# Second routed layer of a graph network on one core: weight loads, bias products, result copies and a norm in other places

## The chip, the cores and the metric

The kernel runs on one core of a Trainium2 chip. The metric is the device time of the whole kernel in microseconds, 5201.13 before the change (median of 3 runs, 5199.01 to 5203.52). A core has five engines that run side by side: TensorE (PE, matmuls and transposes, weights loaded by LDWEIGHTS), VectorE (DVE), ScalarE (ACT), GpSimd (POOL) and SyncE (SP). In this kernel SP issues DMAs only, ACT issues some beside its own work, and POOL issues the indirect ones, which gather rows by a list of indices. Every engine works through its own instructions in order.

## The reference, cut to what matters

Eight layers, alternating graph layers and feed-forward layers, act on 625 nodes of 512 features, each adding to x. The change lies in the fourth, `_L1_ffn_ref`, a routed layer in two levels:

```python
gw = _topk_gate(x @ wg_group, GK, G)              # 2 of 4 groups for each node
z = _layernorm(x, ln_g, ln_b)
out = jnp.zeros_like(x)
for g in range(G):
    iw = _topk_gate(z @ wg_inner[g], EK, E)       # 2 of 8 experts in each group
    moe = jnp.zeros_like(z)
    for e in range(E):
        h = jax.nn.relu(z @ W1[g, e] + b1[g, e])
        moe = moe + iw[:, e:e + 1] * (h @ W2[g, e] + b2[g, e])
    y = _layernorm(z + moe, gln_g[g], gln_b[g])
    out = out + gw[:, g:g + 1] * y
return out.reshape(b, t, d) + inp
```

So each node has four places: two groups, and two experts in each. There are 32 experts, W1 is 512 x 128 and W2 128 x 512 for each, all f32.

## The kernel before, in words

A node is a row; 625 rows are five tiles of 125 (`NT`, `P`). `L1_ffn` has these stages.

Inputs and gates. `C.normed` makes xin, the layer's input; `C.layernorm` makes z, which goes to DRAM as `nodes1` (rows to be gathered). `C.feature_major` (line 166) turns xin and z into xT and zT: four PE transposes a tile into PSUM, and a copy to SBUF that `C.copy` (line 176) gives to DVE and ACT in turn (even tiles DVE, odd tiles ACT). Gate products on xT (pg) and zT (pi), the two best of each (`top8`), and a ranking follow. They give `who` (for every expert a list of up to 128 rows), `to` (where each node finds its four results), and gT, the gates turned so that a product with the biases gives a tile's bias part. A branch (line 1210) on the largest list leads to `L1_late` for lists that are too long; it isn't taken here.

Bias products. For each tile three PE products with gT: one with the norms' biases (line 1223), added to x by DVE (line 1225), after POOL has added xin (line 1224); and for each j, the lower and the upper of a node's two groups, one with b2 (line 1228), added to z by DVE as zb[j] (line 1229). They have 8 or 32 rows of weights and 512 columns.

Experts. Expert e passes through three steps. `places(e)`: rows gathered by POOL (`fetch`, six experts ahead) are transposed by PE (line 1237) and copied to xg (line 1239, ACT). `first(e)`: eight PE matmuls with W1 (line 1249), then relu with bias to hid (line 1251, ACT). `second(e)`: two PE matmuls with W2 to y in PSUM (line 1257), a copy to ys (line 1259, DVE), and a store to `made` in DRAM (line 1260, SP). Each pass of the loop runs `places(e + 1)`, `first(e)`, `second(e - 1)`.

Weights. Four experts' W1, or their W2, are one part of 1 MB; 16 parts pass through a ring of six buffers (`RING`). `load(upto)` issues on SP all parts up to a number. Six are issued ahead of the loop; `first` and `second` ask for more with every expert, which matters at the first of four. A load into a buffer waits on SP until the last matmul that reads the buffer is done.

Results. Once the first 24 experts are stored, `take(0)` gathers the rows of the lower groups on POOL (ten indirect DMAs, line 1269), and `norm(0, ...)` weighs and adds them to zb[0] (line 1280), takes mean and variance (1281, 1282), a square root on ACT, multiplies by the norms' gains from PE (1291, 1292) and adds to x (1293). After the last expert `take(1)` and `norm(1, ...)` do so for the upper groups, in parts of two, two and one tiles, and `C.seen(t)` starts the next layer's norm.

Order. The program's order is the text's, but a scheduler at build time arranges each engine's instructions: one that is ready in its model may be set ahead of earlier ones. In this kernel it set the POOL adds of line 1224 (759.8 us) ahead of the gates, and one gain product of `norm(0)` (844.1 us) ahead of the first expert. Tiles of a name share a number of buffers (`bufs`): xg, hid and ys three each, the PSUM tiles pt, ph, y and pg two each.

Of the kernel before, what the change touches and what calls it, by code (L numbers as in the profile page):

```python
# [15 lines left out]
F32 = mybir.dt.float32  # L16
# [12 lines left out]
N, D, P, NT = 625, 512, 125, 5  # L29
KC = D // 128  # L30
# [10 lines left out]
SLOTS = 128  # L41
RING = 6
# [6 lines left out]
class Ctx:  # L49
# [113 lines left out]
                nc.vector.scalar_tensor_tensor(dst[:, t], src[:, t], mv[:, t, 0:1], g[:P], op0=ALU.subtract, op1=ALU.mult)  # L163
                nc.vector.scalar_tensor_tensor(dst[:, t], dst[:, t], r[:, t:t + 1], b[:P], op0=ALU.mult, op1=ALU.add)

    def feature_major(self, ps, dst, src):

        nc = self.nc
        for t in range(NT):
            pt = ps.tile([128, 512], F32, name="pt")  # L170
            for k in range(KC):
                nc.tensor.transpose(pt[:, k * P:(k + 1) * P], src[:, t, k * 128:(k + 1) * 128],
                                    self.ident[:P, :P])
            self.copy(t, dst[:, :, t * P:(t + 1) * P], pt[:, :KC * P].rearrange("p (k n) -> p k n", k=KC))

    def copy(self, turn, dst, src):

        if turn % 2:
            self.nc.scalar.copy(dst, src)
        else:  # L180
            self.nc.vector.tensor_copy(dst, src)
# [823 lines left out]
def L1_ffn(C):  # L1005
# [7 lines left out]
    nc, tc, I = C.nc, C.tc, C.ins  # L1013
    G, EX, NG = 4, 8, 5
    ALL = G * EX
    W = lambda name: I["L1_ffn_" + name]
    with ExitStack() as st:
# [4 lines left out]
        parts = [(g, q, n) for g in range(G) for q in range(2) for n in ("W1", "W2")]  # L1022
        loaded = {}

        def load(upto):

            for key in parts[len(loaded):upto]:
                g, q, n = key
                w = ring.tile([128, 4, 512], F32, name="ring")
                src = W(n)[g, 4 * q:4 * q + 4]  # L1030
                if n == "W1":
                    nc.sync.dma_start(w, src.rearrange("e (p k) h -> p e (k h)", p=128))
                else:
                    nc.sync.dma_start(w, src.rearrange("e h d -> h e d"))
                loaded[key] = w
# [5 lines left out]
        xin = pool.tile([P, NT, D], F32, name="xin")  # L1041
        C.normed(xin)
        z = pool.tile([P, NT, D], F32, name="z")
# [3 lines left out]
        zT = pool.tile([128, KC, N], F32, name="zT")  # L1047
# [18 lines left out]
        gT = pool.tile([128, N], F32, name="gT")  # L1066

        rb, gb = R([128, D], "rb"), R([128, D], "gb")
# [7 lines left out]
        to = pool.tile([P, 4, NT], U32, name="to")  # L1076
# [4 lines left out]
        def fetch(e):  # L1081
            fetched[e] = at_pool.tile([SLOTS, D], F32, name="at_e")
            nc.gpsimd.indirect_dma_start(out=fetched[e], out_offset=None, in_=nodes[:, :],
                                         in_offset=bass.IndirectOffsetOnAxis(ap=who[:, e:e + 1], axis=0))

        with tc.tile_pool(name="c_ps", bufs=2, space=PSUM) as ps, tc.tile_pool(name="c_x", bufs=1) as xpool:
# [1 line left out]
            wide = R1([P, NT, 4, 32], "wide")  # L1088
            nc.gpsimd.memset(wide, 0.0)
            xT = xpool.tile([128, KC, N], F32, name="xT")  # L1090
            C.feature_major(ps, xT, xin)
            C.feature_major(ps, zT, z)
            wg = pool.tile([128, KC, G], F32, name="wg")
            nc.scalar.dma_start(wg, W("wg_group").rearrange("(k p) g -> p k g", p=128))
            wi = pool.tile([128, KC, G, EX], F32, name="wi")
# [2 lines left out]
            for t in range(NT):  # L1098
                pg = ps.tile([P, G], F32, name="pg", bufs=1)
# [6 lines left out]
            n = NT * NG  # L1106
# [44 lines left out]
            for c in range(4):  # L1151
                for t in range(NT):
                    nc.vector.tensor_scalar(at[:, c, t], slots, rk[:, c, t:t + 1], None, op0=ALU.is_equal)
                    nc.tensor.matmul(pw.rearrange("s h e -> s (h e)"), at[:, c, t], named[:, c, t].rearrange("p h e -> p (h e)"),
                                     start=(c, t) == (0, 0), stop=(c, t) == (3, NT - 1))
# [30 lines left out]
            for t in range(NT):  # L1186
                pt = ps.tile([128, 512], F32, name="pt")
# [25 lines left out]
        work = E(tc.tile_pool(name="c_work", bufs=3))  # L1213
# [3 lines left out]
        ps_g = E(tc.tile_pool(name="c_ps_g", bufs=2, space=PSUM))  # L1217

        zb = [work.tile([P, NT, D], F32, name=f"zb{j}", bufs=1) for j in range(2)]
        for t in range(NT):  # L1220
            cols = slice(t * P, (t + 1) * P)
            po = ps_g.tile([P, D], F32, name="pg")
            nc.tensor.matmul(po, gT[64:64 + 2 * G, cols], gb[64:64 + 2 * G], start=True, stop=True)
            nc.gpsimd.tensor_add(C.x[:, t], C.x[:, t], xin[:, t])
            nc.vector.tensor_add(C.x[:, t], C.x[:, t], po)
            for j in range(2):
                po = ps_g.tile([P, D], F32, name="pg")
                nc.tensor.matmul(po, gT[32 * j:32 * j + 32, cols], rb[32 * j:32 * j + 32], start=True, stop=True)
                nc.vector.tensor_add(zb[j][:, t], z[:, t], po)
        state = {}  # L1230

        def places(e):

            pt = ps_t.tile([128, KC, SLOTS], F32, name="pt")
            rows = fetched.pop(e).rearrange("s (p k) -> s k p", k=KC)
            for k in range(KC):
                nc.tensor.transpose(pt[:, k], rows[:, k], C.ident[:SLOTS, :SLOTS])
            state[e] = work.tile([128, KC, SLOTS], F32, name="xg")
            nc.scalar.copy(state[e], pt)
            if e + 6 < ALL:  # L1240
                fetch(e + 6)

        def first(e):
            g, ex = divmod(e, EX)
            load(parts.index((g, ex // 4, "W1")) + 1 + RING)
            w1 = loaded[g, ex // 4, "W1"]
            ph = ps_h.tile([128, SLOTS], F32, name="ph")
            for k in range(KC):
                nc.tensor.matmul(ph, w1[:, ex % 4, k * 128:(k + 1) * 128], state[e][:, k], start=k == 0, stop=k == KC - 1)
            state[e] = work.tile([128, SLOTS], F32, name="hid")  # L1250
            nc.scalar.activation(state[e], ph, AF.Relu, bias=b1[:, e:e + 1])

        def second(e):
            g, ex = divmod(e, EX)
            load(parts.index((g, ex // 4, "W2")) + 1 + RING)
            y = ps_y.tile([128, D], F32, name="y")
            nc.tensor.matmul(y[:SLOTS], state.pop(e), loaded[g, ex // 4, "W2"][:, ex % 4], start=True, stop=True)
            ys = work.tile([128, D], F32, name="ys")
            nc.vector.tensor_copy(ys[:SLOTS], y[:SLOTS])
            nc.sync.dma_start(made[DENSE + e * SLOTS:DENSE + (e + 1) * SLOTS], ys[:SLOTS])  # L1260

        rows = {}
# [1 line left out]
        def take(j):  # L1264
            rows[j] = [work.tile([P, NT, D], F32, name=f"r{i}", bufs=1) for i in range(2)]
            upto = DENSE + (ALL - EX * (1 - j)) * SLOTS
            for t in range(NT):
                for i in range(2):
                    nc.gpsimd.indirect_dma_start(out=rows[j][i][:, t], out_offset=None, in_=made[:upto, :],
                                                 in_offset=bass.IndirectOffsetOnAxis(ap=to[:, 2 * i + j, t:t + 1], axis=0))  # L1270

        def norm(j, ts):

            a, b = ts[0], ts[-1] + 1
            st_ = C.small.tile([P, NT, 6], F32, name="ln_st")
            mv = C.small.tile([P, NT, 2], F32, name="ln_mv")
            moe = zb[j]
            for t in ts:
                for i in range(2):
                    nc.vector.scalar_tensor_tensor(moe[:, t], rows[j][i][:, t], score[:, 2 * i + j, t:t + 1], moe[:, t], op0=ALU.mult, op1=ALU.add)  # L1280
                nc.vector.bn_stats(st_[:, t], moe[:, t])
                nc.vector.bn_aggr(mv[:, t], st_[:, t])
            v = C.small.tile([P, NT], F32, name="ln_v")
            nc.vector.tensor_scalar_add(v[:, a:b], mv[:, a:b, 1], EPS)
            r = C.small.tile([P, NT], F32, name="ln_r")
            C.rsqrt(r[:, a:b], v[:, a:b], [P, b - a])
            nc.vector.tensor_mul(r[:, a:b], r[:, a:b], wj[:, j, a:b])
            for t in ts:
                gain = ps_g.tile([P, D], F32, name="pg")
                k = 64 + 32 * j  # L1290
                nc.tensor.matmul(gain, gT[k:k + G, t * P:(t + 1) * P], rb[k:k + G], start=True, stop=True)
                nc.vector.scalar_tensor_tensor(moe[:, t], moe[:, t], mv[:, t, 0:1], gain, op0=ALU.subtract, op1=ALU.mult)
                nc.vector.scalar_tensor_tensor(C.x[:, t], moe[:, t], r[:, t:t + 1], C.x[:, t], op0=ALU.mult, op1=ALU.add)

        places(0)
        for e in range(ALL + 1):
            if e + 1 < ALL:
                places(e + 1)
            if e < ALL:
                first(e)  # L1300
            if e:
                second(e - 1)
            if e == ALL - EX + 1:
                take(0)
            if e == ALL - 2:
                norm(0, range(NT))
        take(1)
        for ts in ((0, 1), (2, 3), (4,)):
            norm(1, ts)
# [638 lines left out]


PHASES = [graph_and_L0_gnn, L0_ffn, L1_gnn, L1_ffn, L2_gnn, L2_ffn, L3_gnn, L3_ffn]  # L1950


# [48 lines left out]
```

## Time and profile before

| | us |
|---|---|
| median of three runs | 5201.13 |
| the profiled execution's own time | 5200.93 |
| its span in the profile | 5199.1 |
| layer: end of the layer before to x's last tile | 757.4 to 993.4 |
| PE busy in the whole span | 4803.9 (92%) |
| DVE, ACT, POOL busy | 2679.2, 1098.0, 122.1 |
| DMA, mean over the span | 47 GB/s |

Most of the span is a later layer, a recurrence of 625 steps, which starts after this one is done; the share of busy PE over the whole span therefore says little about this layer. Groups of instructions in the layer: x is the number, us the busy time, ns the mean of one.

| line, engine, what | x | us | ns |
|---|---|---|---|
| 1257 PE y | 64 | 39.5 | 717 |
| 1249 PE ph | 256 | 38.2 | 294 |
| 1237 PE pt | 128 | 22.3 | 300 |
| 1228 and 1223 PE bias products | 20 and 10 | 16.3 and 10.3 | 1132 and 1133 |
| 1259 DVE ys | 32 | 21.8 | 690 |
| 1239 ACT xg | 32 | 18.8 | 587 |
| 1251 ACT hid | 32 | 11.8 | 368 |
| 1083 POOL gathers of rows | 32 | 30.6 | 957 |
| 1269 POOL gathers of results | 20 | 25.0 | 1248 |

A matmul in f32 is two instructions. In the profile's lists, "a <-b" after an idle time names what ended it; a wait row reads: engine, tile and line that waited, what it waited for, us in total, times, the longest. SPq is SP's queue of DMAs, and a DMA's row is the time that SP took to issue it.

### The profile page before, as it was taken

The numbers are of one execution on the slowest core, as the hardware profiler recorded it, in microseconds if no ns is written. First come the engines' busy times: TensorE is split into PE (matmuls) and PEld (weight loads), VectorE is DVE, ScalarE is ACT, GpSimd is POOL, SyncE is SP. The second block draws the span as 40 slices with busy tenths as digits, with TensorE's granted clock in tenths as the row PEclk, the third lists the DMA queues.
The fourth block names the chain that finished last, engine by engine and source line by source line (L and its number), as shares of the span: only waits on it lengthen the run. The fifth ranks groups of instructions, "written<-read, shape, count | busy, mean of one in ns | idle before, by whom it ended". The sixth has DMA issues, their size and how long they took to land. (4 is left out here: it accounts for less than half of the span.)

```text
span 5199.1 us, 184513 instructions
## 1 busy us (share of the span) xinstructions
PE 4803.9 (92%) x74204; PEld 3035.4 (58%) x74204; DVE 2679.2 (52%) x13548; ACT 1098.0 (21%) x4475; POOL 122.1 (2%) x120
## 2 busy tenths in 40 slices
PE   8998977799999799999999999999999999999988
PEld 6566745455567455555555555555555555555555
DVE  7533043400161366666656666665666656656258
ACT  8442111110151111111111111111111111111124
POOL 0100012200000000000000000000000000000000
PEclk9998986799899899999999999999999999999988
DMA  1223954311163100000000000000000000000200
GB/s 38 74 97 128 317 181 163 117 51 47 45 214 124 60 6 6 6 6 6 6 6 13 6 6 6 6 6 6 6 6 6 6 6 6 6 6 0 71 13 11
DMA packets 163039, 246.84 MB, mean 47 GB/s; under 512 B 67001, under 2 KB 67374, under 8 KB 162124
## 3 DMA queue, kind: packets, MB, share of 16 engines
q1 hardware_dynamic: 144480, 221.36, 13.0%
q0 software_dynamic: 8800, 16.92, 1.1%
q10 hardware_dynamic: 9594, 6.59, 0.5%
q8 instruction: 76, 1.25, 0.1%
q14 instruction: 89, 0.73, 0.0%
HBM read 198.90 MB, written 45.91 MB: 47 GB/s over the span
## 5 line engine op out<-in xcount | busy, mean ns | idle before, releaser
L1699 PE MATMUL pa<-wp,left 128*23 128x384 bf16 x33312 | 1499.0, 328 | 126.6 <-issue 38.5
L1699 PEld LDWEIGHTS pa<-wp,left 128*23 128x23 bf16 x33312 | 794.8, 93 | 653.0 <-DVE left L1836 152.1
L1728 PE MATMUL po<-wo,left 128*1 128x128 f32 x20000 | 656.1, 273 | 0.0
L1728 PEld LDWEIGHTS po<-wo,left 128*1 128x1 f32 x20000 | 475.4, 84 | 133.3 <-issue 0.3
L1740 PE MATMUL spare<-wo,ident 128*128 128x256 f32 x1250 | 437.9, 432 | 25.6 <-issue 25.6
L1804 DVE COPY col<-gxb 128x16 f32 x625 | 114.4, 183 | 648.3 <-DVEq L1779 648.3
L1814 DVE STREAM_TRANSPOSE col<-pa 128x384 f32<-128x384 f32 x625 | 349.6, 559 | 190.7 <-PE pa L1699 190.7
L1771 ACT ACTIVATE act<-ga 128x12 f32<-128x12 f32 x625 | 132.6, 212 | 1178.1 <-DVE ga L1816 1178.1
L1766 ACT COPY xrow<-xsb 1x4 f32<-1x4 f32 x625 | 120.5, 193 | 1214.2 <-ACTq L1764 1214.2
L1740 PEld LDWEIGHTS spare<-wo,ident 128*128 128x128 f32 x1250 | 186.2, 188 | 166.3 <-issue 166.3
L1541 PE MATMUL pg<-xT,w 128*128 128x312 f32 (+1 forms) x1024 | 274.4, 429 | 0.8 <-DVE gt L1550 0.3
L1541 PEld LDWEIGHTS pg<-xT,w 128*128 128x128 f32 x1024 | 194.1, 190 | 80.7 <-DVE gt L1550 3.2
L1691 PE MATMUL lg<-wso,th 128*1 128x8 f32 x5008 | 216.1, 169 | 15.5
L1687 PE MATMUL lg<-wsel,act 128*1 128x8 f32 x5008 | 219.2, 169 | 2.1 <-DVE act L1825 0.9
L1818 DVE STREAM_TRANSPOSE col<-po 128x128 f32<-128x128 f32 x625 | 198.2, 317 | 26.6 <-PE po L1728 1.2
L1691 PEld LDWEIGHTS lg<-wso,th 128*1 128x1 f32 x5008 | 148.2, 81 | 74.1 <-DVE wso L1828 13.5
L1684 PEld LDWEIGHTS lg<-xrow,ones 1*1 1x1 f32 x1252 | 51.3, 76 | 238.8 <-issue 238.8
L502 PE MATMUL wide<-hot_dst,hot_src 125*125 125x512 bf16 x640 | 177.0, 389 | 13.3 <-DVE hot_dst L482 12.9
L1828 DVE TENSOR_TENSOR wso<-wsel,so 128x32 f32<-128x32 f32 x625 | 120.3, 192 | 117.6 <-ACT so L1773 115.9
L1687 PEld LDWEIGHTS lg<-wsel,act 128*1 128x1 f32 x5008 | 149.4, 81 | 48.1 <-DVE act L1825 3.3
L232 PE MATMUL po<-w,hT 128*125 128x512 f32 x400 | 175.1, 592 | 0.0
L1773 ACT ACTIVATE so<-go 128x4 f32<-128x4 f32 x625 | 128.3, 205 | 216.8 <-DVE go L1823 216.8
(495 smaller groups left out, 5905.4 us busy)
## 6 DMA issues: line engine op xcount, KB each, us to landing
ring<-in_L_ffn_W_dram SPq DMA_DIRECT2D x80, 1024.0 KB
gxb<-gx SPq DMA_DIRECT2D x25, 800.0 KB
w<-in_L_ffn_WihT_dram SPq DMA_DIRECT2D x16, 1024.0 KB
raw<-in_L_ffn_WhhT_dram SPq DMA_DIRECT2D x24, 512.0 KB
gx<-gt SPq DMA_DIRECT2D x16, 626.0 KB
made<-ys SPq DMA_DIRECT2D x39, 256.0 KB
gx<-gt SPq DMA_DIRECT2D x16, 624.0 KB
w<-in_L_gnn_Wl_dram SPq DMA_DIRECT2D x8, 1024.0 KB
```

Of the source, the lines that this page charges most:

```text
L232: self.nc.tensor.matmul(out, xT[:, k, t * P:(t + 1) * P], w[:, k, :], start=start and k == 0, stop=stop and k == k_n - 1)
L502: nc.tensor.matmul(wide[i], hs[:, k], hd[:, :W0], start=first, stop=last)
L1541: nc.tensor.matmul(pg[:, :n], w[:, k, s * 128:(s + 1) * 128], xT[:, k, n0:n0 + n], start=k == 0, stop=k == KC - 1)
L1687: pe.matmul(lg, c2[:, s:s + 1], wsel[:, 1, s], start=False, stop=False)
L1691: m = pe.matmul(lg, th[:, s:s + 1], wso[:, s], start=False, stop=s == KC - 1)
L1699: m = pe.matmul(pa[32 * j:32 * j + 2 * GAP + 1], upper[:, s], wp[e][:, s, i, j].rearrange("p g n -> p (g n)"), start=k == 0, stop=k == 11, ...
L1728: m = pe.matmul(po[32 * j:32 * j + 1].rearrange("p (u r) -> p u r", r=32), left[:, s, 0:1], wo[e][:, s].rearrange("p (u j r) -> p j u r", ...
L1740: pe.matmul(spare[:, :256], C.ident, wo[0][:, 0, :256], start=True, stop=True)
L1771: act.activation(act4[:, 0:3].rearrange("p g s -> p (g s)"), ga, AF.Tanh, scale=0.5).then_inc(sem["ifg"])
L1773: act.activation(so, go, AF.Sigmoid).then_inc(sem["so"])
L1814: dve.transpose(col[:, :12, :32], pa.rearrange("p (b r) -> p b r", r=32)).then_inc(sem["ta"])
L1818: dve.transpose(col[:, 12:, :32], po.rearrange("p (s r) -> p s r", r=32)).then_inc(sem["to"])
```

## The change

- `load` is asked for `RING - 1` in place of `1 + RING` parts beyond the number of the part in use: at part number i, parts up to i + 4 are issued where it was up to i + 6.
- The bias products become a function `inputs(i)` that does one product; the loop calls it once in each pass from e = 2 to 16, after `second`. The order within a tile is b2 of both j first, then the norms' biases.
- The copy to ys goes from DVE to ACT, the copy to xg from ACT to DVE; xg has two buffers in place of three, ys four in place of three.
- The ten copies of `feature_major` in this layer are all on ACT.
- `norm(0, range(NT))` becomes `norm(0, (0, 1))` at the same place and `norm(0, (2, 3, 4))` after the last `second`.

```diff
-    def feature_major(self, ps, dst, src):
+    def feature_major(self, ps, dst, src, copy=None):
...
-            self.copy(t, dst[:, :, t * P:(t + 1) * P], pt[:, :KC * P].rearrange("p (k n) -> p k n", k=KC))
+            to, of = dst[:, :, t * P:(t + 1) * P], pt[:, :KC * P].rearrange("p (k n) -> p k n", k=KC)
+            copy(to, of) if copy else self.copy(t, to, of)
...
-            C.feature_major(ps, xT, xin)
-            C.feature_major(ps, zT, z)
+            C.feature_major(ps, xT, xin, nc.scalar.copy)
+            C.feature_major(ps, zT, z, nc.scalar.copy)
...
-        for t in range(NT):
+
+        def inputs(i):
+            t, what = divmod(i, 3)
             cols = slice(t * P, (t + 1) * P)
             po = ps_g.tile([P, D], F32, name="pg")
-            nc.tensor.matmul(po, gT[64:64 + 2 * G, cols], gb[64:64 + 2 * G], start=True, stop=True)
-            nc.gpsimd.tensor_add(C.x[:, t], C.x[:, t], xin[:, t])
-            nc.vector.tensor_add(C.x[:, t], C.x[:, t], po)
-            for j in range(2):
-                po = ps_g.tile([P, D], F32, name="pg")
+            if what == 2:
+                nc.tensor.matmul(po, gT[64:64 + 2 * G, cols], gb[64:64 + 2 * G], start=True, stop=True)
+                nc.gpsimd.tensor_add(C.x[:, t], C.x[:, t], xin[:, t])
+                nc.vector.tensor_add(C.x[:, t], C.x[:, t], po)
+            else:
+                j = what
                 nc.tensor.matmul(po, gT[32 * j:32 * j + 32, cols], rb[32 * j:32 * j + 32], start=True, stop=True)
                 nc.vector.tensor_add(zb[j][:, t], z[:, t], po)
...
-            state[e] = work.tile([128, KC, SLOTS], F32, name="xg")
-            nc.scalar.copy(state[e], pt)
+            state[e] = work.tile([128, KC, SLOTS], F32, name="xg", bufs=2)
+            nc.vector.tensor_copy(state[e], pt)
...
-            load(parts.index((g, ex // 4, "W1")) + 1 + RING)
+            load(parts.index((g, ex // 4, "W1")) + RING - 1)
...
-            load(parts.index((g, ex // 4, "W2")) + 1 + RING)
+            load(parts.index((g, ex // 4, "W2")) + RING - 1)
...
-            ys = work.tile([128, D], F32, name="ys")
-            nc.vector.tensor_copy(ys[:SLOTS], y[:SLOTS])
+            ys = work.tile([128, D], F32, name="ys", bufs=4)
+            nc.scalar.copy(ys[:SLOTS], y[:SLOTS])
...
             if e:
                 second(e - 1)
+            if 2 <= e < 17:
+                inputs(e - 2)
             if e == ALL - EX + 1:
                 take(0)
             if e == ALL - 2:
-                norm(0, range(NT))
+                norm(0, (0, 1))
+            if e == ALL:
+                norm(0, (2, 3, 4))
```

## The prediction

> **What bounds the kernel now.** I read the page first, then cut the second routed layer into four stretches, then read its chain of work in order of time, last its table of waits and the DMA queue's own waits. The layer's last result (x of the fifth tile) stands at 993.4 us of a span of 5199.1; everything after it waits for x, so what the layer saves, the kernel saves. The four stretches run from the last norm of the layer before (757.4), the first row transposes after the branch (824.65), the expert loop (842.42) and the last store of an expert's result (957.9):
>
> ```profile
> 757.40:824.65 67.25, 36.72 (x156) 29.37 (x156) 45.60 (x221) 4.76 (x10) 15.34 (x17) 0.52 0.48 148
> 824.65:842.42 17.77, 16.57 (x25) 6.07 (x26) 8.48 (x13) 0.00 (x0) 0.00 (x0) 0.50 0.00 1
> 842.42:957.90 115.48, 91.45 (x455) 64.39 (x455) 34.26 (x58) 32.03 (x66) 36.62 (x36) 0.84 0.73 241
> 957.90:993.40 35.50, 13.08 (x15) 3.56 (x13) 29.86 (x98) 1.20 (x7) 12.89 (x10) 0.50 0.31 88
> ```
>
> Columns: length, busy time of PE, weight load, DVE, ACT, POOL, granted clock, DMA share, GB/s. The second stretch is nothing but bias products, with DMA idle. In the third PE is idle 24 us and its clock falls. Where the loop is smooth, an expert takes 2.22 us (857.92 to 860.15 to 862.37):
>
> ```profile
> 857.92 1.02 PE L1257 MATMUL y<-ring,hid 128*128 128x512 f32 x2
> 858.78 0.63 PE L1237 MATMUL pt<-ident,at_e 128*128 128x128 f32 x4
> 859.25 1.06 PE L1249 MATMUL ph<-xg,ring 128*128 128x128 f32 x8
> 860.15 1.02 PE L1257 MATMUL y<-ring,hid 128*128 128x512 f32 x2
> ...
> 862.37 1.02 PE L1257 MATMUL y<-ring,hid 128*128 128x512 f32 x2
> ```
>
> 32 x 2.22 is 71 us, not 115. The waits of the loop say why:
>
> ```profile
> DVE ys L1259 <- DMA made<-ys: 42.5, 10, 12.5
> PE y L1257 <- DVE ys L1259: 18.7, 8, 6.1
> SPq L1260 <- DVE ys L1259: 89.4, 20, 38.3
> SPq L1034 <- PE y L1257: 17.1, 4, 7.8
> SPq L1032 <- PE ph L1249: 12.7, 5, 4.9
> ```
>
> The copy of y waits 42.5 us for an earlier store to leave its buffer. Stores and weights share SP's queue, and a weight load stands there until the block that now uses its ring buffer is done (12.7 and 17.1 us). Seen in time:
>
> ```profile
> 864.79 0.38 SPq L1032 DMA_DIRECT2D ring<-in_L_ffn_W_dram  x1
> 873.03 0.38 SPq L1034 DMA_DIRECT2D ring<-in_L_ffn_W_dram  x1
> 873.51 1.77 SPq L1260 DMA_DIRECT2D made<-ys  x3
> ```
>
> Three stores stand behind the load of 873.03. (Of the 89.4 us, 38.3 are only the wait for the first result.)
>
> **What the skill says.** "DMA: Bandwidth & Descriptors", section "Anatomy of one DMA — SWDGE (gpsimd) path": a semaphore wait is made on the issuing sequencer before dispatch. The trace agrees: everything behind the waiting load is late. Same page, "Issuing engines are not separate DMA queues": transfers of all queues share 16 engines. It agrees: from 858 to 866 loads, stores and row gathers fill them (share 0.97, 325 GB/s). "ScalarE: Activation LUTs", section "Table sets: the hidden batching unit": relu and copy lie in every set, so copies cost no table load. It agrees: the layer has one load for Exp and one for Sqrt, none for Relu or copy. "TensorE: Matmul & The Clock Gate", section "What's actually happening": the clock is halved unless PE has been busy; it agrees (0.50 at 825 to 842, 1.00 at 858 to 866), with a twist used below.
>
> **The change, part by part**, against the profiled execution: 5200.93 us, that is 1.8 outside its span, and 0.2 under the median 5201.13.
>
> Loads. Place q used to ask for the part six ahead, into the buffer in use; now four ahead, into the buffer of two places before, which the last instructions have just freed. The load starts at the same moment as before, but SP no longer stands on it. Nothing is loaded later. With one more result buffer (4), the 42.5 us wait loses its cause. What stays is the store's own way: the one issued at 859.4 behind two loads of 1 MB still held a buffer until about 870.1, some 10.7 us. Four buffers at 3.1 us each (below) give 12.4. It just fits while bias products are in the loop; at 2.22 us (8.9) it is short by 2 to 3 us in the last two blocks that load. The loop's traffic, 28.35 MB at about 330 GB/s (full 8 us windows move 303 to 398), is 86 us, so DMA is a near second bound. I put 6 us for both.
>
> Bias products. 15 products and 15 DVE adds leave the stretch before the loop: -17.8 us. They run in experts 2 to 16. At full clock a pair of 512-column matmuls takes PE 0.86 us (two 0.43 steps, as in y: 858.78 less 857.92). I take three as still ahead of the loop, where PE waits for rows anyway: 12 x 0.87 = +10.4. Experts then take 2.22 + 0.87 = 3.09. Their 0.69 us adds and the 0.69 us xg copies make 1.38 of 3.09 us on DVE: hidden by PE; if not, 15 x 0.69 = 10.
>
> Copies. ys goes DVE to ACT (0.69 to 0.59, same shape as xg), xg goes ACT to DVE (0.59 to 0.69). ACT keeps 0.37 + 0.59 = 0.96 us an expert: hidden, net 0. But ACT is in order: a ys that waits for its buffer now holds the next hid.
>
> Transposes' copies. DVE gives five or six copies of 0.68 us (3 xT, 3 zT) to ACT. PE stood at 764.5 to 773.7 for an xT copy that DVE made at 772.94; four of the five gate products (1.8 us each, 7.2) ran after z was begun. If they come before z, up to 7.2 us go, and the rest of the copies' 2 us; if ACT's DMA issues hold them (four of wi took 766.77 to 771.06), nothing. -5 us; from +2 to -9.
>
> Norm in two parts. Per tile 2 x 0.75 + 0.68 + 0.17 + 0.73 + 0.75 = 3.8 us, 19 us in all; the split adds six small operations of 0.17, 1.0 us, and one 0.2 square root. What moves is who stands behind it. Before, the last two ys copies came at 956.55, after norm(0)'s sums, which waited for gathered rows (to 953.17), though PE's last y was issued by 949.5. Now ys is on ACT and escapes; but xg of the last experts, and ACT behind the square root, can stand behind such a wait. I leave 4 us.
>
> The sum: loop = first two experts at half clock 9.0 (842.42 to 851.4 today) + 31 x 2.22 = 68.8 + 10.4 + 4 + 6 + 1.3 for the last copy and store = 99.5 against 115.5. Stretches: 62.2 + 0 + 99.5 + 37.5 (2 us since norm(0) ends later relative to the second gathers; ten gathers at 1.5 us on POOL and 25 us of DVE otherwise as now) = 199.2 against 236.0. That is -36.8: 5200.93 - 36.8 = 5164.1.
>
> **Rivals.**
> (a) The products stay ahead of the loop, since the order on each engine is set at build time and work is hoisted: L1291, of expert 30 in the program, ran at 844.12 before expert 0. Then -17.8 + 10.4 is lost, and experts at 2.22 us meet the traffic, some 6 us more: a gain of 23, 5178. Against: rows are wanted first in program order now.
> (b) Store latency, not SP's order, is the limit: a wait of 3 us more on ACT in each of five loading blocks, 15 us, a gain of 22, 5179. For: DMA at 0.9 to 1.0 most of the loop. Against: 10.7 is under 12.4.
> (c) More: everything overlaps (prelude -9, no leftover 6 and 4): a gain of 51, 5150.
> (d) Slower: the products use 8 or 32 of 128 rows, and 825 to 842 shows PE busy 16.6 of 17.8 us with the clock still 0.50. If a product an expert keeps the clock there, 15 experts cost 3.09 us more, +46, and the sum turns to +9: 5210. It decides from 12 experts at half clock (12 x 3.09 = 37). Against: between 906 and 914 PE is busy 6.13 of 8 us and the clock stays 1.00, and 842 to 851 warms up with one such product inside.
>
> **How the numbers follow.** Likeliest 0.60 (its own range 5153 to 5174), (a) 0.17, (b) 0.12, (c) 0.06, (d) 0.05, of which 0.04 slower. 0.2% is 10.4 us, about what a measurement of this kernel tells from no change: faster 0.94, same 0.02, slower 0.04. The range takes in (a), (b) and most of (c), and the unknown of the prelude: 5142 to 5187.
>
> **What would show it.** Right: no loads' waits on SP, the ys wait for stores under 12 us in total, bias products between experts at 1.0 clock, the loop begun some 20 us earlier, x ready near 957. Wrong: ACT ys waiting long for stores (b); products in one row before the first expert (a); a clock of 0.5 in experts 2 to 16 (d); xg copies on DVE late behind zb sums; a changed time after the layer, which nothing here explains.

## The result, and the profile after

The changed kernel takes 5171.96 us (median of 5 runs, 5169.16 to 5177.47) against 5201.13 (median of 5 runs, 5197.98 to 5204.65, on the same chip): ratio 0.9946, 95% interval 0.9935 to 0.9958, or 29 us faster. The forecast was 5164, its likeliest case 5153 to 5174, so the sign, the size and the time are as foretold; the layer gave 34.8 of the 36.8 us, and 4.1 us were lost just behind it. Why the forecast held, and how much of that was luck, is taken up below. The profiled execution took 5170.27 us, its span is 5168.5.

The stages of the layer after the change, in the same view and columns as the four stretches of before. There are now three: the stretch of bias products is gone, and the loop follows the first row transposes.

```profile
758.86:818.92 60.06, 33.31 (x154) 26.04 (x155) 41.20 (x214) 8.10 (x16) 15.36 (x17) 0.55 0.52 161
818.92:923.20 104.28, 95.72 (x480) 63.26 (x481) 41.99 (x70) 31.60 (x66) 37.42 (x36) 0.93 0.81 270
923.20:960.00 36.80, 12.35 (x15) 3.12 (x13) 31.31 (x106) 1.56 (x8) 13.17 (x10) 0.53 0.29 84
```

The loop took 115.48 us with PE idle for 24 of them at a clock of 0.84; it is now 104.28 us with PE idle for 8.6, at 0.93, though the bias products are inside. DMA's share went from 0.73 to 0.81: about the same bytes (27.8 and 28.2 MB) in less time.

The waits of the layer from the first row transposes on, and those of SP's queue, as before (engine, tile and line that waited, for what, us in total, times, longest):

```profile
PE ph L1254 <- DVE xg L1244: 7.7, 1, 7.7
...
ACT ys L1264 <- DMA made<-ys: 5.9, 3, 3.4
```

```profile
SPq L1035 <- PE y L1262: 7.4, 3, 2.5
...
SPq L1033 <- PE ph L1254: 5.5, 5, 1.6
```

The wait of the result copy for earlier stores fell from 42.5 us in 10 to 5.9 in 3; all three lie between 891 and 900 us, well after the last bias product (875). Loads still stand on SP: 12.9 us in these two rows, where the same two had 29.8, and none longer than 2.5 where it was 7.8. A new wait of PE for xg (7.7 us) has come up at the loop's end.

In time, from the PE rows of the smooth part, where one product lies in each expert:

```profile
839.50 1.02 PE L1262 MATMUL y<-ring,hid 128*128 128x512 f32 x2
840.46 1.12 PE L1232 MATMUL pg<-rb,gT 32*125 32x512 f32 x2
841.50 0.75 PE L1242 MATMUL pt<-ident,at_e 128*128 128x128 f32 x4
842.09 1.06 PE L1254 MATMUL ph<-xg,ring 128*128 128x128 f32 x8
842.98 1.02 PE L1262 MATMUL y<-ring,hid 128*128 128x512 f32 x2
```

An expert with a product takes 3.48 us (839.50 to 842.98), 1.26 more than the 2.22 without; the forecast had put 0.87.

### The profile page after: what moved, and what is told of

Its sections match the earlier page's. It is cut to its first block, busy times and chain, and to the rows that moved or that the text cites. A ratio compares the mean times of both kernels' runs of the same rounds, so it can differ in the third digit from the quotient of the medians.

```text
span 5168.5 us, 184510 instructions
## 1 busy us (share of the span) xinstructions
PE 4789.0 (93%) x74204; PEld 3029.9 (59%) x74204; DVE 2675.0 (52%) x13549; ACT 1102.6 (21%) x4482; POOL 123.2 (2%) x120
```

## The experiments

Stage lengths tell more here than the kernel's time, since the later recurrence of 625 steps, whose text is not touched, took between 3084 and 3102 us in the profiles of these fourteen builds (3089.4 before, 3087.1 after). Each kernel's stages, in us: A from the layer's start to the first row transposes, B from there to x of the last tile, C from there to the next layer's first aggregation. Medians of the kernel before lay between 5196.7 and 5201.1 in these runs, so times are given as ratios to it.

```
                              A      B     C     median us  ratio to before [95%]
before                       67.4  168.5  14.2   5201.1
after                        60.1  141.1  18.3   5172.0     0.9946 [0.9935, 0.9958]
loads undone                 60.0  147.6  18.3   5173.7     0.9960 [0.9946, 0.9973]
bias products undone         62.9  149.1  18.3   5179.6     0.9968 [0.9955, 0.9980]
swap of copies undone        63.2  141.5  14.2   5165.9     0.9940 [0.9926, 0.9953]
transposes' copies undone    65.4  141.6  19.2   5184.2     0.9976 [0.9966, 0.9985]
norm in one part             63.7  141.4  19.0   5170.4     0.9944 [0.9931, 0.9958]
loads alone                  68.5  161.6  18.9   5210.3     1.0020 [1.0013, 1.0026]
buffers alone                67.7  168.6  14.2   5207.3     1.0010 [1.0002, 1.0018]
sums held back               63.1  138.6  18.5   5169.3     0.9941 [0.9927, 0.9954]
held back, row buffers       63.6  136.2  18.2   5166.7     0.9938 [0.9925, 0.9952]
gate weights first           60.2  140.4  21.6   5169.0     0.9946 [0.9932, 0.9959]
five products over 128 rows  60.4  136.8  18.2   5169.4     0.9939 [0.9925, 0.9953]
all additions together       65.4  130.8  15.3   5156.9     0.9912 [0.9899, 0.9926]
```

Some numbers of A, about 60 in some and about 63 in others, belong to kernels whose text is the same up to there. In those at 60 PE's clock was above 0.50 for part of the gate products (0.58 to 0.67 from 777 to 787 us); of the others it was so only in the one with the products ahead of the loop. So a difference of 3 us in A is put down to no edit. The changed kernel is one of those at 60; why they differ was not found.

### One part undone

**Loads.** `load(... + 1 + RING)` in both places, as before; all else as changed.

> The changed kernel with the loads asked for six parts ahead again, all else as changed. Theory (SP's order): SP stands on each load until the block in use is done, stores stand behind it, ys waits for its buffer, now on ACT, and hid behind it; PE stalls in each of the five loading blocks. Layer 201 us becomes about 216 (210 to 226), the ys wait for stores 5.9 us becomes 20 to 45, kernel about 5187. Rival (the engines of DMA are full and set the pace, whoever issues first): the layer stays within 4 us of 201, kernel 5170 to 5176.

B is 6.5 us longer, 147.6. That is between the two, nearer the rival: the loads' order is worth 6.5 us once the rest of the change is in, not the whole stall. The result copy waits 7.6 us for stores, not 20 to 45, although SP stands 17.4 us on loads (12.9 after the change). As long as a product lies in each expert no y is late: all of them follow at 3.48 us, as in the changed kernel. The longest wait of the copy, 5.8 us from 889.5 on, comes after the last product and costs some 4 us; the rest is lost at the loop's end. So four buffers and the longer turn cover SP's standing on a load by themselves; its order matters where the turn is 2.22 us.

**Bias products.** All fifteen ahead of the loop again, with loads, copies and buffers as changed:

```diff
+        for t in range(NT):
+            for what in (2, 0, 1):
+                inputs(3 * t + what)
         places(0)
...
-            if 2 <= e < 17:
-                inputs(e - 2)
```

> The changed kernel with all 15 bias products ahead of the first expert again, all else as changed. A product takes 1.26 us of the loop in the changed kernel (3.48 against 2.22 us an expert), so 12 of them 15.1, and stood for 17.8 ahead of the loop. Theory (the products also cover DMA): experts at 2.22 us meet 4 MB a block, ys waits for stores 2 to 3 us in each of five blocks, and the layer grows by 2.7 + 10 to 15 us, to about 214, kernel 5185. Rival (order is all): only the 2.7 us come back, layer 204, kernel 5175.

B is 8.0 us longer, between the rival's 2.7 and the theory's 12.7 or more. The waits of this kernel bear out the theory's cause; they show what the products' time was covering:

```profile
ACT ys L1264 <- DMA made<-ys: 27.1, 12, 4.1
```

Without products the y of the first fourteen experts follow at 2.22 us, and then five of the next fourteen come at 2.9 to 3.9, because ACT waits for stores. From the first W1 products to the last store it is 91.5 us here, and 100.1 with the products between. So twelve products, which take 15.1 us of PE, make the loop only 8.6 us longer, and they take 16.8 from ahead of it (first transposes to first W1 products, 21.2 us here against 4.4).

**Swap of copies.** ys on DVE and xg on ACT as before, with the new numbers of buffers:

```diff
-            nc.vector.tensor_copy(state[e], pt)
+            nc.scalar.copy(state[e], pt)
...
-            nc.scalar.copy(ys[:SLOTS], y[:SLOTS])
+            nc.vector.tensor_copy(ys[:SLOTS], y[:SLOTS])
```

> The changed kernel with ys copied by DVE and xg by ACT as before, four ys and two xg buffers kept. Theory: the loop's middle is the same to 1 us; at the end the last ys stand behind the sums of the lower groups on DVE instead of xg, so the 7.7 us wait of PE for xg goes but the last stores come later; layer +4 us (0 to +8), kernel 5176. Rival (ACT's order matters in the whole loop, since a waiting ys holds hid): the middle gets shorter, layer -3 us, kernel 5169.

B differs by 0.4 us, so the swap is worth nothing here. As the theory had it, PE's wait for xg is gone, but now the ys copies stand behind the sums on DVE, and the last store comes no earlier (104.4 us after the first transposes against 104.6). C falls back to 14.2, which is taken up below.

**Transposes' copies.** `C.feature_major(ps, xT, xin)` and the same for z, without `nc.scalar.copy`.

> The changed kernel with the copies of the ten transposes given to DVE and ACT in turn. Theory: the stretch from the layer's start to the branch was 67.2 us and is 60.1; all of the 7.1 comes from these copies: layer +7 us (5 to 9), kernel 5179, loop unchanged. Rival (part of it comes from the bias products that no longer stand in front of the branch): +3 us, kernel 5175.

A is 5.3 us longer and B within 0.6 (141.6): the part acts ahead of the loop. Its worth is less sure. The clock in this kernel's gate products was 0.50, so that it belongs with the kernels at 63, and against those it is 2 us longer. The part is thus worth 2 to 5 us, and theory and rival are not told apart.

**Norm in two parts.** `norm(0, range(NT))` after expert 29, and nothing after the last.

> The changed kernel with the lower groups' norm in one part again (all five tiles at once, asked for after expert 29). Theory, the split hardly matters: six small DVE operations and a square root fewer (about 1.2 us), but the first norm and the products behind it begin only when all ten gathers of the lower groups are in; the layer is 199 to 203 us against 201.1, the kernel within 4 us of the changed one. Rival, the split is what keeps more sums of the lower groups from standing on DVE ahead of the last xg copies: PE's wait for xg grows from 7.7 us to 12 or more and the layer to 206 or more.

B differs by 0.3 us and PE's wait for xg is 7.6 us, as with the split: it brings nothing in these runs.

### One part alone

> The kernel before with only the loads' change: each place of the loop asks for the part four ahead (into the buffer just freed) in place of six ahead. Three result buffers and three xg buffers stay, the bias products stay ahead of the loop, the copies stay as they were. Theory, the order on SP was the cause of the 42.5 us that DVE waited for stores: the wait falls under 15 us, the layer of 236.0 us becomes 212 to 218, the kernel about 5178. Rival, a store's own way behind 1 MB loads (about 10 us against three buffers of 2.22 us) is the cause: more than 25 us of the wait stay, the layer is within 8 us of 236, the kernel 5191 to 5199.

```diff
-            load(parts.index((g, ex // 4, "W1")) + 1 + RING)
+            load(parts.index((g, ex // 4, "W1")) + RING - 1)
...
-            load(parts.index((g, ex // 4, "W2")) + 1 + RING)
+            load(parts.index((g, ex // 4, "W2")) + RING - 1)
```

The waits of this kernel, first of the result copy, then of SP for the loads:

```profile
DVE ys L1259 <- DMA made<-ys: 29.8, 7, 4.7
```

```profile
SPq L1034 <- PE ph L1249: 0.3, 1, 0.3
SPq L1032 <- PE ph L1249: 0.3, 1, 0.3
SPq L1032 <- PE y L1257: 0.2, 1, 0.2
```

SP hardly stands on a load any more (0.8 us in these three rows, where before had 29.8 in the two that were shown), yet 29.8 of the 42.5 us wait for stores stay, as the rival had it, and B is 6.9 us shorter, not 20. The wait has only changed its cause: the PE rows show every second expert late. Three buffers at 2.22 us are 6.7 us, which is less than the 10.7 us read for a store's own way before the change.

```profile
871.33 1.02 PE L1257 MATMUL y<-ring,hid 128*128 128x512 f32 x2
...
874.73 1.10 PE L1257 MATMUL y<-ring,hid 128*128 128x512 f32 x2 [1.01 <-DVE ys L1259]
...
877.03 1.02 PE L1257 MATMUL y<-ring,hid 128*128 128x512 f32 x2
...
880.40 1.10 PE L1257 MATMUL y<-ring,hid 128*128 128x512 f32 x2 [0.98 <-DVE ys L1259]
```

The kernel is 10 us slower than before although the layer is 5.9 us shorter: C is 4.7 longer, and the recurrence takes 3102.1 us in the profile (3089.4 before). Neither theory had that. The profiled execution was the slowest of 21 (5217.65 against a median of 5210.33), so its recurrence is longer than usual.

> The kernel before with only the numbers of buffers of the change: four for the results (ys) in place of three, two for the gathered rows (xg) in place of three. The loads still ask six ahead. Theory, the order on SP is the cause: a store that stands 8 us behind a load stalls four buffers too, each of some ten waits is at most 2.2 us shorter, the layer is 0 to 10 us shorter than 236.0. Rival, the number of buffers against a store's own way is the cause: the wait of 42.5 us falls under 15, the layer is 15 to 25 us shorter, the kernel about 5180.

```diff
-            state[e] = work.tile([128, KC, SLOTS], F32, name="xg")
+            state[e] = work.tile([128, KC, SLOTS], F32, name="xg", bufs=2)
...
-            ys = work.tile([128, D], F32, name="ys")
+            ys = work.tile([128, D], F32, name="ys", bufs=4)
```

```profile
DVE ys L1259 <- DMA made<-ys: 27.9, 3, 12.2
```

B is 168.6 us, the same to a tenth, as the theory had it. The wait is three stalls of up to 12.2 us in place of ten: with SP standing on a load, a fourth buffer only lets PE run on a little before the same load holds it.

So loads alone give 7 us of B, buffers alone none, and loads, buffers, swap and split norm together, without the products, 19.4 (168.5 to 149.1). Swap and split are worth nothing when undone, which leaves order and buffers together as the likely cause. That pair by itself was not run, nor was the changed kernel with three ys buffers.

### What ends the layer

The end of the loop after the change, in the rows of PE and then of DVE:

```profile
903.73 0.63 PE L1242 MATMUL pt<-ident,at_e 128*128 128x128 f32 x4
912.04 2.08 PE L1254 MATMUL ph<-xg,ring 128*128 128x128 f32 x8 [7.67 <-DVE xg L1244]
```

```profile
908.47 0.77 DVE L1285 SCALAR_TENSOR_TENSOR zb<-r,score,zb 125x512 f32<-125x512 f32 x1 [8.45 <-DMA r<-made,to]
910.63 0.75 DVE L1285 SCALAR_TENSOR_TENSOR zb<-r,score,zb 125x512 f32<-125x512 f32 x1 [1.40 <-DMA r<-made,to]
911.30 0.68 DVE L1244 COPY xg<-pt 128x512 f32<-128x512 f32 x1
```

The rows for expert 29 were transposed by 904.4, but their copy stands on DVE behind two sums that wait for gathered results (908.47 and 910.63). PE waits 7.67 us, and its clock is low for what follows (eight matmuls take 2.08 us, which took 1.06). Two kernels take this away:

```diff
+                held = work.tile([P, 1], F32, name="held", bufs=1)
+                nc.vector.tensor_scalar(held, state[ALL - 1][:P, 0, 0:1], 0.0, None, op0=ALU.mult)
+                for i in (0, 2):
+                    nc.vector.tensor_scalar(score[:, i], score[:, i], held, None, op0=ALU.add)
                 norm(0, (0, 1))
```

> The changed kernel, with the lower groups' scores made to depend on the last expert's gathered rows (one small DVE product and two small additions of zero), so that no sum of the lower groups can stand on DVE ahead of the last xg copies, where in the changed kernel one of them held xg of expert 29 for 7.67 us. Theory, two nearly tied ends: the wait of PE for xg goes (7.7 to under 1 us) and the last store comes some 7 us earlier after the first row transposes (104.6 to about 97), but the upper groups' gathers still wait until the lower groups' last sum has freed the row buffers (923.8 in the changed kernel, against 923.2 for the store), and those sums now start later; the layer gains 0 to 3 us of 201.1. Rival, the wait for xg alone sets the end: the layer is 7 to 8 us shorter, about 193.5, and the kernel about 5164.

> As the run before (no sum of the lower groups ahead of the last xg copies), and with a row buffer for each tile of nodes in place of one for all five, so that the gathers of the upper groups wait only for the sum of their own tile. Theory, two nearly tied ends: now both are gone, the store is some 7 us earlier and the gathers follow it at once; the layer is 6 to 9 us shorter than 201.1, about 193.5, the kernel about 5164. Rival, the end is bound by the gathers' own row on POOL (20 of 1.5 us) or by DVE's 25 us of sums and norm: the layer stays within 3 us of 201.

```diff
-            rows[j] = [work.tile([P, NT, D], F32, name=f"r{i}", bufs=1) for i in range(2)]
+            rows[j] = [[work.tile([P, D], F32, name=f"r{i}{t}", bufs=1) for t in range(NT)] for i in range(2)]
```

Holding back the sums moves the last store 9.2 us forward (95.4 us after the first row transposes in place of 104.6), but x only 2.5: the upper groups' gathers start at 926.34 us, 9.2 us after that store was issued (917.1), 0.3 us behind the lower groups' sum of 925.30, which was late because it was held back. With a row buffer for each tile B is 4.9 us shorter, 136.2, short of the 6 to 9 of the theory: the gathers start at 924.39, still 7.3 us behind the last store (917.1 here too), where it was 2.7 in the changed kernel. Up to then the lower groups' own gathers, issued until 921.1, fill the DMA engines together with that store (share 0.87 to 0.99 from 912 to 921 us); that they make it late was not tried. Shown is that the 7.7 us wait and the row buffers are nearly tied, so that removing the wait alone gives a third of it.

### The next layer's start

The PE row of the next layer's gate product in the changed kernel, where none waited before:

```profile
968.83 3.52 PE L233 MATMUL pg<-gw,xT 128*125 128x4 f32 x16 [3.70 <-DMA gw<-in_L_gnn_gate_W_dram]
```

The issues in order of time, first in the kernel before, then in the changed one:

```profile
992.86 0.38 ACTq L1366 DMA_DIRECT2D gw<-in_L_gnn_gate_W_dram  x1
993.16 0.33 SPq L210 DMA_DIRECT2D m_mean<-graph_mean  x1
```

```profile
959.38 0.33 SPq L211 DMA_DIRECT2D m_mean<-graph_mean  x1
959.45 0.41 ACTq L1375 DMA_DIRECT2D gw<-in_L_gnn_gate_W_dram  x1
```

In the three kernels where the small gw was issued 0.30 us ahead of the graph C is 14.2 (before, swap undone, buffers alone). In the nine others with gw on ACT's queue it was issued from 0.02 us ahead to 0.36 us behind, PE waits 3.6 to 4.6 us for it, and C is 18.1 to 19.2. What the change did is to shift two queues against each other by 0.4 us.

```diff
+        gw = pool.tile([128, KC, EX], F32, name="gw")
+        nc.sync.dma_start(gw, W("gate_W").rearrange("(k p) e -> p k e", p=128))
         m = C.load_graph(pool, "mean")
...
-            gw = pool.tile([128, KC, EX], F32, name="gw")
-            nc.scalar.dma_start(gw, W("gate_W").rearrange("(k p) e -> p k e", p=128))
```

> The changed kernel, with the next layer's small gate weights (gw) asked for on SP ahead of its 1.37 MB graph (m_mean), in place of ACT's queue 0.07 us behind it. Theory, the next layer's first product waits for gw only because the large load was issued first: from the last x of the routed layer to the first aggregation of the next 14 us, as in the kernel before, in place of 18.3; the kernel is some 4 us shorter, about 5167. Rival, the added wait comes from what else is in flight there (or from the graph itself): 18 us stay and the time stays at 5171.

Neither: C is 21.6. PE's wait for gw is gone, but the next small load behind the graph, wx (issued at 958.76), now holds DVE, where its product stands ahead of the last copies of xT:

```profile
971.34 0.18 DVE L1500 TENSOR_SCALAR wx<-wx 128x32 f32<-128x32 f32 x1 [9.79 <-DMA wx<-in_L_ffn_WselT_dram]
```

```profile
972.41 3.52 PE L233 MATMUL pg<-gw,xT 128*125 128x4 f32 x16 [6.12 <-DVE xT L182]
```

The mechanism holds (wx, issued 0.91 us behind the large load, lands 12.6 us after its issue), but the cure was half of one.

### What a product costs

```diff
-                nc.tensor.matmul(po, gT[64:64 + 2 * G, cols], gb[64:64 + 2 * G], start=True, stop=True)
+                nc.tensor.matmul(po, gT[:, cols], gb, start=True, stop=True)
```

> The changed kernel, with the five products of the group gates (what == 2) made over all 128 rows of gT and gb, whose other rows are zero, in place of 8 rows; the other ten stay at 32 rows. Theory, the 0.4 us that a product costs beyond its 0.86 comes from the change of the number of rows of the weights before and after it (the load of the weights is not drawn ahead): experts with such a product take about 3.09 us from one y to the next, those with a product of 32 rows still 3.48, and the layer is 1.5 to 2 us shorter. Rival, any product between the experts costs 1.26 (two matmuls more, each with its own weights and wait): 3.48 us for all, the layer within 1 us of 201.1.

One PE trace holds both kinds:

```profile
833.92 1.02 PE L1262 MATMUL y<-ring,hid 128*128 128x512 f32 x2
834.87 1.12 PE L1232 MATMUL pg<-rb,gT 32*125 32x512 f32 x2
...
837.40 1.02 PE L1262 MATMUL y<-ring,hid 128*128 128x512 f32 x2
838.26 1.02 PE L1227 MATMUL pg<-gb,gT 128*125 128x512 f32 x2
...
840.48 1.02 PE L1262 MATMUL y<-ring,hid 128*128 128x512 f32 x2
```

3.48 us with 32 rows, 3.08 with 128. An expert with a product of 8 rows takes 3.48 too in the changed kernel; here the same product has 120 rows more, which meet zeros among the biases, and takes 0.40 us less. At full rows a product costs the 0.86 of the forecast. The weight loads (PEld) of the same stretch show where the time goes:

```profile
834.87 0.29 PEld L1232 LDWEIGHTS pg<-rb,gT 32*125 32x125 f32 x2 [0.76 <-issue]
835.92 0.56 PEld L1242 LDWEIGHTS pt<-ident,at_e 128*128 128x128 f32 x4 [0.76 <-issue]
...
837.83 0.19 PEld L1227 LDWEIGHTS pg<-gb,gT 128*125 128x125 f32 x1 [0.24 <-issue]
```

With 32 rows the weights are loaded only at the product's own start (834.87), and those of the transposes behind it only at theirs (835.92). With 128 rows they are loaded at 837.83, 0.43 us ahead of the product, beside the matmuls of y. So the late load that the theory names is seen in the trace.

B falls by 4.3: four experts by 0.4 are 1.6; 2.4 more come before the first y (5.8 us after the first transposes in place of 8.2), where PE reached full clock earlier. Whether the wider product did that isn't shown; the kernel with all additions, which has it too, needs 7.3 us.

### All additions together

Held-back sums, row buffers, gw first, all products over 128 rows, and the two products of late small loads on GpSimd:

```diff
-            nc.vector.tensor_scalar_mul(wx_1, wx, -KEPT)
+            nc.gpsimd.tensor_scalar_mul(wx_1, wx, -KEPT)
...
-            nc.vector.tensor_scalar_mul(bsel[:, 1], bsel[:, 0], 1.0 - KEPT)
+            nc.gpsimd.tensor_scalar_mul(bsel[:, 1], bsel[:, 0], 1.0 - KEPT)
```

> The changed kernel with four additions: all bias products over 128 rows (other rows zero; the gathered rows' queue is five deep in place of six and hid has two buffers, to make room), no sum of the lower groups ahead of the last xg copies, a row buffer for each tile of nodes, and in the next layer the small gate weights asked for ahead of the 1.37 MB graph, with the two products of small late loads (wx, bsel) made by GpSimd in place of DVE. Theory: an expert with a product takes 3.09 us in place of 3.48 (12 x 0.4 = 4.7), the end of the loop gives 3 to 5, so that the layer is 192 to 194 in place of 201.1; from x to the next layer's aggregation 14 to 15 us in place of 18.3, since nothing on DVE or PE stands behind a small load that came after the large one; the kernel is 5157 to 5161. Rival, the wait moves on again (to DMA in the loop, to another small load after it): the kernel stays at 5166 to 5171.

5156.89 us, ratio 0.9912 [0.9899, 0.9926], under both kernels. B is 10.2 us shorter than in the changed kernel, every expert with a product takes 3.08 us, and C is 15.3, with no gate product waiting for gw:

```profile
956.48 6.73 PE L233 MATMUL pg<-gw,xT 128*125 128x4 f32 x32
```

A is 5.3 us longer (65.4), so that the layer is 196.2, above the 192 to 194 of the theory. The stages give 4.9 + 3.0 = 7.9 us of the 15 by which the medians differ; in the profile (19.8 us shorter, since this execution was faster than its median) the rest lies ahead of the layer and after the next layer's first aggregation, where none of the additions was meant to act.

## Why the prediction was right, point by point

**Transposes' copies (-5, from +2 to -9).** Within the range: 2 to 5.3. A fell by 7.4 in all; some 3 us of it go with the higher clock of the gate products, which the forecast did not have, and which kernels with the same text up to there lack. That the stretch came out near the forecast (60.1 against 62.2) is in part luck. (PE stood for the xT copy from 765.6 on, for 8.1 us, not from 764.5.)

**Bias products out of their stretch (-17.8).** 16.8 (21.2 to 4.4 us from the first transposes to the first W1 products). Three stayed ahead, as assumed, so rival (a) fell. Of the fifteen, twelve had stood in this stretch; the other three had run ahead of the branch, from 816.5 us on, which the forecast did not count apart.

**Bias products in the loop (12 x 0.87 = 10.4).** The term of the sum that was mis-sized: 12 x 1.26 = 15.1. The count, the place and the clock were right (1.00 among the products, against rival (d)); the duration came from a pair of 512-column matmuls with 128 rows of weights, and these have 8 or 32. The run with five full-row products shows 0.86 for those. The forecast says that a clock of 0.50 from 825 to 842 us agrees with a clock that is halved unless PE has been busy. It doesn't: PE was busy 16.6 of those 17.8 us, as the forecast's own rival (d) says. What kept the clock there was not tried.

**Loads and buffers (the 42.5 us loses its cause; 6 left).** The outcome was right, 5.9 us on ACT and about 0.6 of it in the spacing of y. The step behind it was half right. The forecast made SP's order the cause and the fourth buffer an aid against the store's own 10.7 us. Loads alone brought 7 us of B, buffers alone none; and with the loads as before but buffers and products as changed, the wait is 7.6 us, hardly more than 5.9. So, as far as these runs show, SP's order was one cause of the 42.5 us, and the number of buffers times the time of a turn the other. Its other sentence, that 10.7 fits four buffers at 3.1 us an expert but not at 2.22, was borne out by the kernel with the products ahead of the loop: 27.1 us of waits. Rival (b), the store's way as the limit, thus shows as soon as buffers or products are missing. "No loads' waits on SP" was wrong: 12.9 us stay, waits for PE's products of the buffer's former part, which were not done when its load was asked for.

**Swap of copies (0).** Right: 0.4.

**End of the loop (4 us for xg behind sums).** Right in kind, too small: 9.8 us (the spacing of the last four y, less 2.22 each).

**The tail (37.5).** 36.8. The norm's split, counted at +1.2, is within 0.3 of nothing.

**The sum.** Loop: 8.2 to the first y + 68.8 + 15.1 + 0.6 + 9.8 + 1.7 for the last copy and store = 104.2, measured 104.3, forecast 99.5. The two undersized terms (4.7 and 5.8) outweigh the 5.4 that stores did not take. Layer: 60.1 + 104.3 + 36.8 = 201.2 against 199.2. The layer's 2 us are closer than its terms: errors of 4.7 to 5.8 us of opposite sign cancel, and that is luck.

**After the layer.** "A changed time after the layer, which nothing here explains" is what came: +4.1 us for gw. In the profile: start +1.4, layer -34.8, next layer's start +4.1, the rest -1.3, together the 30.6 by which the span fell. That the rest moved so little is luck too, since the untouched recurrence differs by up to 18 us between these builds. The forecast had taken x as the only thing for which the next layer waits.

## What to carry to other kernels

Look at the order on a queue and the number of buffers behind it together. Here the buffers times the time of a turn had to cover a store's way to memory, some 10.7 us with the time behind two loads: 3 x 2.22 = 6.7 us left 29.8 us of waits (loads alone), 4 x 2.22 = 8.9 left 27.1 (products undone), and 4 x 3.48 = 13.9 left none as long as the products lasted. Mending order or buffers alone brought 7 us and none, both together 19.4 with the swap and the split in. Where an end has been moved, look at what is issued there on different queues, since a shift of 0.4 us between a small and a large load decided over 4 us, and moving one load moved the wait to the next. Read the price of an instruction from a row with the same number of weight rows, in the same company.

## What was not expected of the hardware

- A matmul pair of 512 columns between pairs of 128-row weights costs 1.26 us with 8 or 32 rows of weights and 0.86 with 128 rows (zeros added). The rows above show the weights of such a product, and those of the transposes behind it, loaded only when they start. Whether the small number of rows or its change from one product to the next does that isn't told apart; the transposes, which have 128 rows themselves, speak for the change.
- The same recurrence took 3084.2 to 3102.1 us in the profiles of fourteen builds, 0.005 to 0.03 us a step between the two that were changed on the kernel before by loads or buffers alone (3102.1 and 3097.6) and the others (3084.2 to 3094.6). Over 21 and 13 runs those two kernels stayed slower than before (ratio 1.0020 and 1.0010), so it isn't one slow execution. In their profiles PE waits for a tile of DVE (`left`) 79 times, 12.1 us in all, and 63 times, 9.7 us, where it was 27 times and 4.1 us before. The cause was not settled.
- A small load that was issued from 0.02 us ahead of a 1.37 MB one to 0.36 us behind it kept PE waiting for about 4 us; 0.30 us ahead it was in time, and one issued 0.9 us behind landed after 12.6 us.
